# A triangle multiplication's b projection that takes tokens side by side, and a new issue order

## The chip, the cores and the metric

One core of a Trainium2 chip runs the whole program in one launch. The time is the device time of one execution in microseconds (us). In the trace the engines are PE (TensorE's matmuls), PEld (its weight loads), DVE (VectorE), ACT (ScalarE), POOL (GpSimd) and SP (SyncE, which here only issues transfers). L873 means line 873 of the kernel before.

## What is computed

Two layers over `x` of shape (32, 56, 56, 128), that is 32 images of 56 x 56 tokens with 128 channels, all float32:

```python
# layer 0
x = x + conv3x3(sign(batchnorm(_ln_c(x))), sign(W) * mean|W|)     # 128 -> 128 channels
t = x as (32, 3136, 128)
t = t + moe(_ln_t(t))               # router to 8 experts, best 2, softmax gates, 128 -> 128 each
# layer 1
x = x + triangle(_ln_c(x))
t = t + expert_choice(_ln_t(t))     # 64 experts; each takes its best 8 tokens of every image

def triangle(x):
    a = sigmoid((x @ Wa1 + ba1) * (x @ Wa2 + ba2))     # 128 -> 16
    b = sigmoid((x @ Wb1 + bb1) * (x @ Wb2 + bb2))     # 128 -> 16
    g = sigmoid(x @ Wg + bg)
    z = einsum('bikc,bkjc->bijc', a, b)                # rows of a by columns of b, per channel
    return g * (_ln(z) @ Wz + bz)
```

The change lies in the computation of `b` in `triangle`; the rest matters because it shares the engines.

## The kernel before

**Tiling.** Images go in 16 pairs. A pair's 2 x 56 rows are cut into 7 units of 16 rows (896 tokens), held as [128 partitions, 7, 128 channels] in float32. A row has 56 columns, counted as column = 7 v + n with v from 0 to 7 and n from 0 to 6: a partition holds the seven columns n of one (row, v). Turned (channels on partitions), a pair's normalised tokens lie in one buffer, `yT` [128, n = 7, row = 112, v = 8]. So, along a partition, the eight columns v of a row are neighbours, and a whole image of one n is 448 numbers in a row; a single column v over all rows has a step of eight numbers.

**Stages.** A first phase reads all of `x`, normalises, sums for the batch norm and loads the weights. Then each pair goes through these stages, at the names the trace uses:

- convolution: SP fetches `x` and `ys`; DVE writes signs into `frame` (L609); PE runs nine taps of 448 columns (`ps_cv`, L631); ACT scales (`cv`, L639); PE turns it back (`trc`); DVE adds;
- mixture of experts: statistics on DVE (`st`, then small steps ending in `rm`); ACT normalises (`ym`); PE turns (`trm`); ACT copies (`xT`); the router (`ps_rl`, `ps_r`) and its gates on DVE; PE turns the gates (`trg`), ACT copies and stores them to memory. For each of the seven blocks of a unit SP fetches the gates back, spread over all partitions (`gb`, 512 KB), DVE multiplies them onto the tokens (L825), and PE runs eight matmuls into `acc` (L830); DVE adds;
- triangle: statistics (`rmln`), ACT's norms (`yt`), PE's turn (`trt`), ACT's copies into `yT`; `tri_b` and `tri_a`; `tri_z`, the product per channel (`ps_z`, L972), its norm, and a way through memory into `zc`; `tri_out` with the gate matmuls (`ps_g`, L1063) and the output projection (`ps_zo`, L1085);
- expert choice: statistics, norms (`yl`), turn (`trl`), copies, logits (`ps_l`, ACT's copy of 128 x 448), DVE's MAX8 over all tokens of an image, index search, ACT's exponential over the logits (`top8`), the gathers on GpSimd. The experts' own matmuls and the scatters into the output (L1497, GpSimd) come when all pairs are through; only a part of them starts earlier.

**The projections a and b.** `gated_half` (L861 to L914) does one half (h = 0, 1) of one of them. For each of the two images it fills one PSUM bank: four matmuls (g = 0 to 3), each with the 128 x 32 weights into its own 32 partitions, 392 columns each. For `a` the moving operand is seven rows with all their columns, for each of the seven n a run of 7 x 8 = 56 neighbours. For `b` it is one column, v = 2 g + h, of all 56 rows and all seven n: 392 numbers eight apart. ACT adds the bias and writes the bank into `lines` (L882 for b, L887 for a), which lie as [(g, two times 16 channels), 7 slices, both images' rows at 0 and 64]. PE turns the seven slices (`tr_b`, `tr_a`; four into one bank and three into another); ACT copies the second factor (`abm`, L905), DVE multiplies it with the first (L910). Last, ACT's sigmoid writes `b_s` (L927) or `a_bd` (L945), the two operands of `ps_z`. So b has 2 halves x 2 images x 16 pairs = 64 banks and as many line copies; a has the same.

**What sets the order.** Nothing is left to the compiler's scheduler. Every operation is recorded with its engine, a planned cost in ns, what it reads and what it writes (`@op`). Its rank is the pair's number times 14 plus a number of the table `TICK` (L38 to L67), one number for each stage and unit. `Order.run` then plays the program in planned time: at each moment each engine takes, of the operations whose operands are ready by the plan and whose buffers are free, the one with the lowest rank. The instructions are issued in the order so found. On the chip each engine works through its own list strictly in that order. A changed cost or rank can thus move operations of any stage. The rotating buffers have fixed numbers: 8 PSUM banks, 12 of `x`, 5 of `u` (`ys`, `cv`, `ym`, `yt`, `yl`, `sg` and others share them), 5 of `gb`, 3 of `yl` (the turned `yl`), 2 of `abm`.

The sums that a mean over channels needs in the load of the weights use `mean_w`, a 128 x 128 matrix of 1/128 (L323, L324); it is read at L1775 and L1795.

Of the kernel before, what the change touches and what calls it, by code (L numbers as in the profile page):

```python
# [12 lines left out]
F32 = mybir.dt.float32  # L13
# [3 lines left out]
AF = mybir.ActivationFunctionType  # L17
# [21 lines left out]
    "fetch": (1.02, -3.61, 2.69, -0.51, 1.44, 9.95, 12.41),  # L39
    "sign": (-0.5, 1.65, 2.33, 6.44, 7.89, 10.12, 11.51),  # L40
    "conv": (2.3, 3.61, 7.1, 8.56, 10.24, 11.55, 14.66),
    "conv_back": (2.64, 3.67, 7.29, 8.6, 10.28, 12.05, 15.19),
    "moe_turn": (5.91, 4.92, 9.12, 9.24, 12.92, 12.75, 15.53),
    "moe_gates": (6.45, 6.7, 9.47, 10.57, 13.11, 13.01, 16.67),
    "moe_experts": (7.02, 7.48, 9.81, 10.77, 13.79, 15.45, 17.23),
    "moe_add0": (9.01, 10.3, 10.03, 12.99, 16.15, 17.26, 18.81),
    "moe_add1": (7.58, 10.23, 12.34, 12.06, 15.46, 16.15, 18.8),
    "tri_turn": (15.5, 16.45, 18.46, 17.26, 19.45, 19.21, 19.35),
    "moe_stats": (4.04, 8.64, 12.23, 15.22),
    "moe_route": (6.38, 9.37, 13, 15.78),  # L50
    "tri_stats": (14.95, 13.48, 18.14, 19.08),
    "tri_b": (19.69, 19.75),
    "tri_a": (19.7, 20.48),
    "tri_z": (21.12,),
    "tri_out": (23.16, 24.17, 24.33, 25.06, 26.73, 27.48, 29.06),
    "gate_stats": (24.67, 24.78, 28.01, 30.57),
    "gate_turn": (25.36, 25.49, 26.93, 28.7, 29.36, 30.77, 32.34),
    "gate_logits": (25.97, 26.82, 27.76, 30.12, 31.49, 34.49, 33.31, 33.27),
    "clear": (33.53,),
    "top8": (35.12,),  # L60
    "pool_rows": (35.94,),
    "late_first": (36.84, 37.89, 39.05, 42.18, 42.2, 42.46),
    "late_alone": (45.47, 44.2, 38.54, 42.56, 42.9, 46.32),
    "late_rest": (37.49, 37.53, 39.21, 40.16, 41.64, 41.88, 42.22, 43.47, 46.56, 47.54),
    "last_sums": (47.77,),
    "last_rows": (52.37,),
# [217 lines left out]
def kernel(ctx: ExitStack, tc: tile.TileContext, a: dict, out: bass.AP):  # L284
# [38 lines left out]
    mean_w = const.tile([128, 128], F32, name="mean_w")  # L323
    nc.gpsimd.memset(mean_w, 1.0 / C)  # L324
# [80 lines left out]
    with ExitStack() as c2:  # L405
# [18 lines left out]
        lines = [one.tile([128, N7, 128], F32, name=f"lines_{h}") for h in range(2)]  # L424
# [433 lines left out]

        all_rows = [("yT", u, n0) for u in range(NU) for n0 in (0, 4)]

        def gated_half(p, x, h, pieces, w, bias):  # L861

# [1152 lines left out]
```

## Time and profile before

| quantity | value |
|---|---|
| time, median of three runs | 3907.89 us (3904.44 to 3908.85) |
| time of the profiled execution | 3864.27 us |
| its span, first to last instruction | 3862.1 us |
| mean granted clock of TensorE in it | 0.960 |
| instructions in it | 78172 |
| experts' matmuls `acc` (L830) | 12544, 1462.6 us busy, 278 ns each |
| convolution taps `ps_cv` (L631) | 2016, 433.1 us, 361 ns each |
| gate products `gb` on DVE (L825) | 784, 952.9 us, 1223 ns each |
| norms `yt`, `yl`, `ym` on ACT (L560) | 784 each, 335.1, 329.4 and 315.5 us |
| scatters into the output (L1497) | 128, 198.1 us, 1548 ns each |
| memory traffic | 811.90 MB in packets, 209 GB/s over the span |

The span and all rows below it are of one profiled execution. The slices quoted below divide the span into 40 equal stretches; a digit is the busy share in tenths. A line of the timeline gives the start in us, the duration of a run of like instructions, engine, line, operation, output and inputs by name, the shape, the number of instructions, and in brackets the idle time of that engine before it with what ended it. In a line of the stretches, start and end are followed by the length, and each engine's busy us with the number of its instructions.

### The profile page before, as it was taken

The numbers are of one execution on the slowest core, as the hardware profiler recorded it, in microseconds if no ns is written. First come the engines' busy times: TensorE is split into PE (matmuls) and PEld (weight loads), VectorE is DVE, ScalarE is ACT, GpSimd is POOL, SyncE is SP. The second block draws the span as 40 slices with busy tenths as digits, with TensorE's granted clock in tenths as the row PEclk, the third lists the DMA queues.
The fourth block names the chain that finished last, engine by engine and source line by source line (L and its number), as shares of the span: only waits on it lengthen the run. The fifth ranks groups of instructions, "written<-read, shape, count | busy, mean of one in ns | idle before, by whom it ended". The sixth has DMA issues, their size and how long they took to land.

```text
span 3862.1 us, 78172 instructions
## 1 busy us (share of the span) xinstructions
PE 3515.1 (91%) x27693; PEld 2833.9 (73%) x27693; DVE 3142.5 (81%) x10452; ACT 2353.3 (61%) x5458; POOL 409.8 (11%) x472
## 2 busy tenths in 40 slices
PE   7999999999999999999999999999999999997673
PEld 6886787777777777777777778786868787865342
DVE  7997879898989898989898989898989898875310
ACT  5997446665756566666657575757575747565210
POOL 1000000000000000000000000000010101013657
PEclk8999999999999999999999999999999999987776
DMA  7996547565656565555556555655556565556784
GB/s 247 351 353 245 214 165 247 171 236 180 227 188 213 198 209 197 203 208 207 201 204 212 204 209 202 207 203 214 204 198 220 191 227 188 207 191 190 196 212 69
DMA packets 325542, 811.90 MB, mean 210 GB/s; under 512 B 86169, under 2 KB 110658, under 8 KB 325154
## 3 DMA queue, kind: packets, MB, share of 16 engines
q1 hardware_dynamic: 262034, 680.39, 51.2%
q10 hardware_dynamic: 41104, 109.20, 7.2%
q0 software_dynamic: 22016, 17.32, 3.0%
q8 instruction: 220, 3.60, 0.4%
q14 instruction: 168, 1.38, 0.1%
HBM read 630.19 MB, written 176.55 MB: 209 GB/s over the span
## 4 chain that ended last, share of the span: by engine, by line
PE 43%; DVE 20%; ACT 18%; DMA 13%; issue 3%; POOL 2%; SPq 0%; ACTq 0%; POOLq 0%; DVEq 0%
PE acc L830 28%; DMA gb<-gate 7%; DVE stln L486 5%; DMA out<-eo_False,picked 5%; ACT yt L560 3%; DVE sg L1098 3%; DVE gb L825 2%; PE ps_cv L631 2%; PE gram L1673 2%; DVE x L1107 2%; POOL out L1497 2%; ACT y L560 2%; ACT cv L639 2%; PE ps_z L972 2%; ACT ym L560 2%
## 5 line engine op out<-in xcount | busy, mean ns | idle before, releaser
L830 PE MATMUL acc<-expert_w,gb 128*128 128x128 f32 x12544 | 1462.6, 278 | 45.6 <-DVE gb L825 43.8
L830 PEld LDWEIGHTS acc<-expert_w,gb 128*128 128x128 f32 x12544 | 1434.2, 194 | 71.5 <-DVE gb L825 62.8
L825 DVE TENSOR_TENSOR gb<-gb,xT 128x1024 f32<-128x1024 f32 x784 | 952.9, 1223 | 95.6 <-DMA gb<-gate 93.2
L486 DVE BATCH_NORM_STATS2 stln<-x 128x6 f32<-128x128 f32 x2352 | 576.6, 287 | 1.5
L560 ACT ACTIVATE yt<-x,rmln 128x128 f32<-128x128 f32 x784 | 335.1, 493 | 212.6 <-DVE rmln L548 205.1
L631 PE MATMUL ps_cv<-frame,w_sign 128*128 128x448 bf16 x2016 | 433.1, 361 | 8.4 <-DVE frame L609 8.4
L560 ACT ACTIVATE yl<-x,rmln 128x128 f32<-128x128 f32 x784 | 329.4, 488 | 167.3 <-DVE rmln L545 157.3
L631 PEld LDWEIGHTS <-w_sign 128*128 128x128 bf16 x2016 | 193.2, 99 | 222.5 <-issue 66.5
L560 ACT ACTIVATE ym<-x,rmln 128x128 f32<-128x128 f32 x784 | 315.5, 485 | 56.7 <-DVE rmln L548 55.8
L1229 POOL DMA_INDIRECT rows<-y,near x128 | 124.1, 969 | 1148.5 <-PE trt L475 1040.7
L1114 POOL MEMSET a_bd<- 128x2048 f32 x16 | 29.5, 1842 | 1818.7 <-PE ps_zo L1085 1818.7
L1497 POOL DMA_INDIRECT out<-eo_False,picked x128 | 198.1, 1548 | 143.3 <-DMA out<-eo_False,picked 79.9
L581 ACT COPY xT<-trm 128x512 f32<-128x512 f32 x224 | 108.2, 536 | 163.4 <-PE trm L475 129.5
L639 ACT ACTIVATE cv<-ps_cv,cv_shift,cv_scale 128x448 f32<-128x448 f32 x224 | 159.5, 720 | 77.8 <-PE ps_cv L631 58.7
L560 ACT ACTIVATE y<-x,rm 128x128 f32<-128x128 f32 x448 | 194.8, 486 | 19.5 <-DVE rm L545 11.3
L1063 PE MATMUL ps_g<-wg,yT 128*128 128x128 f32 x1568 | 200.9, 280 | 0.0
L842 DVE TENSOR_TENSOR x<-acc,x 128x512 f32<-128x512 f32 x224 | 139.7, 624 | 74.5 <-PE acc L830 74.2
L486 DVE BATCH_NORM_STATS2 st<-x 128x6 f32<-128x128 f32 x784 | 180.6, 282 | 23.2 <-DMA x<-in_x 22.8
L1673 PE MATMUL gram<-y 128*128 128x128 f32 x1568 | 197.3, 278 | 0.0
L1673 PEld LDWEIGHTS gram<-y 128*128 128x128 f32 x1568 | 193.2, 199 | 0.0
L1063 PEld LDWEIGHTS ps_g<-wg,yT 128*128 128x128 f32 x1568 | 187.2, 194 | 8.2 <-PE pe_False L1471 0.8
L475 PE MATMUL tr<-ident,y 128*128 128x128 f32 x784 | 138.6, 294 | 27.5 <-ACT y L560 23.7
(244 smaller groups left out, 5305.4 us busy)
## 6 DMA issues: line engine op xcount, KB each, us to landing
gb<-gate SPq DMA_DIRECT2D x784, 512.0 KB
x<-in_x SPq DMA_DIRECT2D x224, 448.0 KB
y<-yT SPq DMA_DIRECT2D x112, 448.0 KB
ys<-y SPq DMA_DIRECT2D x112, 448.0 KB
out<-x ACTq DMA_DIRECT2D x112, 448.0 KB
y<-yl ACTq DMA_DIRECT2D x112, 448.0 KB
w_False<-in_L_ffn_weight SPq DMA_DIRECT2D x128, 256.0 KB
w_True<-in_L_ffn_weight SPq DMA_DIRECT2D x48, 256.0 KB
```

The source lines that it names most:

```text
L475: nc.tensor.transpose(ps.ap[:, n * 128 : (n + 1) * 128], get()[:, n0 + n, :], ident)
L486: nc.vector.bn_stats(st.ap[:, c0 + k, :], src.ap[:, k, :])
L560: nc.scalar.activation(dst.ap[:, k, :], src.ap[:, k, :], AF.Identity, bias=m, scale=r)
L631: nc.tensor.matmul(acc, lhsT=w_sign[:, tap, :], rhs=frames[f][:, 8 * band + kh : 8 * band + kh + 8, kw : kw + W], start=(tap == 0), stop=( ...
L639: nc.scalar.activation(cv.ap[:, :, 64 * h : 64 * h + 64], ps.ap[:, :448].rearrange("c (q n) -> c n q", n=N7), AF.Identity, bias=cv_shift, ...
L825: nc.vector.tensor_tensor(gb.ap, gb.ap, over(xT.ap[:, n, :], E0), ALU.mult)
L830: nc.tensor.matmul(acc.ap[:, n % 4 * C : (n % 4 + 1) * C], lhsT=gb.ap[:, e, :], rhs=expert_w[:, e * C : (e + 1) * C], start=(e == 0), stop ...
L842: nc.vector.tensor_tensor(dst, acc.ap[:, : k * C], dst, ALU.add)
L1063: nc.tensor.matmul(psg.ap[:, n * C : (n + 1) * C], lhsT=yT[:, n0 + n, 16 * u : 16 * u + 16, :].rearrange("c r v -> c (r v)"), rhs=wg, star ...
L1229: nc.gpsimd.indirect_dma_start(out=rows.ap[:, j, :], out_offset=None, in_=y3_d[p], in_offset=bass.IndirectOffsetOnAxis(ap=near.ap[:, k + j ...
L1497: ins = nc.gpsimd.indirect_dma_start(out=tokens_out, out_offset=bass.IndirectOffsetOnAxis(ap=picked[lot][:rows, e : e + 1], axis=0), in_=e ...
L1673: nc.tensor.matmul(gram.ap[:, :C], lhsT=y.ap[:, n, :], rhs=y.ap[:, n, :], start=(g % G16 == 0 and n == 0), stop=(g % G16 == G16 - 1 and n ...
```

## The change

The changed kernel computes the same. Five things differ.

1. **b's pieces.** Half h of b now takes the residues n = 4 h + g: four for h = 0, three for h = 1. One matmul takes all 448 neighbouring tokens of one n and one image. So the bank has 448 columns, in the second half on 96 partitions only. `lines` grow from 7 to 8 slices (one for each v), the turn makes four and four, `abm` holds [8, 4, 16]; the sigmoid writes the columns n = 0 to 3 or 4 to 6 of every v. The piece for g = 3 has its place on the array given explicitly. `a` keeps its form.
2. **`mean_w`** leaves the constants and becomes an operation of the weights' load in a buffer of the `yl` kind.
3. **Planned costs**: those of the projections (twice the columns plus 60 on PE, the columns plus 60 on ACT), the turns (20 + 130 k for k slices, instead of 125 k), `ps_z` (1880 for 1776), `ps_g` (40 more), `ps_zo` (680 for 900), `ps_l` (890 for 800), and one activation of the late experts (1850 for 1800).
4. **The table `TICK`** has new numbers throughout.
5. From costs and table, `Order.run` yields another order on every engine. In the steady state, for example, MAX8 stands ahead of the last step of unit 6's norm statistics on DVE, four `ps_l` stand ahead of the pair's last experts on PE, and 36 convolution matmuls instead of 18 stand ahead of the experts of units 2 and 3.

```diff
 TICK = {
...
-    "conv": (2.3, 3.61, 7.1, 8.56, 10.24, 11.55, 14.66),
+    "conv": (2.4, 3.69, 6.8, 7.72, 10.43, 11.89, 12.86),
...
-    "moe_experts": (7.02, 7.48, 9.81, 10.77, 13.79, 15.45, 17.23),
+    "moe_experts": (7.18, 7.67, 10.31, 10.83, 14.93, 12.94, 16.8),
...
-    "tri_b": (19.69, 19.75),
-    "tri_a": (19.7, 20.48),
-    "tri_z": (21.12,),
+    "tri_b": (19.79, 19.99),
+    "tri_a": (19.82, 21.57),
+    "tri_z": (21.72,),
...
-    "top8": (35.12,),
+    "top8": (34.46,),
...
-    mean_w = const.tile([128, 128], F32, name="mean_w")
-    nc.gpsimd.memset(mean_w, 1.0 / C)
...
-        lines = [one.tile([128, N7, 128], F32, name=f"lines_{h}") for h in range(2)]
+        lines = [one.tile([128, NV, 128], F32, name=f"lines_{h}") for h in range(2)]
...
-        def turned(src, name, keys=None, get=None):
+        def turned(src, name, keys=None, get=None, pieces=((0, 4), (4, 3))):
...
-            for n0, k in ((0, 4), (4, 3)):
+            for n0, k in pieces:
                 ps = bank(f"{name}_{n0}")
 
-                @op("PE", k * 125, r=keys or parts(src)[n0 : n0 + k], w=[ps])
+                @op("PE", 20 + k * 130, r=keys or parts(src)[n0 : n0 + k], w=[ps])
...
-        def gated_half(p, x, h, pieces, w, bias):
+        def gated_half(p, x, h, w, bias):
...
-            cols = x == "b"
             name = f"{x}_{p}_{h}"
+            if x == "a":
+                n_i, groups, size = N7, 4, 392
+            else:
+                n_i, groups, size = NV, (4, 3)[h], 448
+            rows = 32 * groups
             for img in range(2):
                 ps = bank(f"ps_{name}_{img}")
 
-                @op("PE", 830, r=all_rows, w=[ps])
+                @op("PE", 2 * size + 60, r=all_rows, w=[ps])
                 def _(ps=ps, img=img):
-                    for g in range(4):
+                    for g in range(groups):
+                        if x == "a":
...
+                        else:
+                            piece = yT[:, 4 * h + g, H * img : H * img + H, :].rearrange(
+                                "c r v -> c (r v)"
+                            )
+                            to = ps.ap[32 * g : 32 * g + 32, :size]
                         nc.tensor.matmul(
-                            ps.ap[32 * g : 32 * g + 32, :392].rearrange("s (n k) -> s n k", n=N7),
-                            lhsT=w, rhs=pieces(img, g), start=True, stop=True,
+                            to, lhsT=w, rhs=piece, start=True, stop=True,
+                            **({"tile_position": (0, 96)} if g == 3 else {}),
                         )
 
-                @op("ACT", 460, r=[ps], w=[("lines", h, img)])
+                @op("ACT", 60 + size, r=[ps], w=[("lines", h, img)])
...
+                        of = ps.ap[:rows, :size].rearrange("s (r v) -> s v r", v=NV)
+                    nc.scalar.activation(to, of, AF.Identity, bias=bias[:rows])
+
+            u = new("abm", [128, NV, 4, CH], f"abm_{name}")
...
-            u = gated_half(
-                p, "b", h,
-                lambda img, g: yT[:, :, H * img : H * img + H, 2 * g + h],
-                wb, bb,
-            )
+            u = gated_half(p, "b", h, wb, bb)
 
             @op("ACT", 540, r=[(u, 0), (u, 4)], w=[(b_s, h)])
             def _():
+                ns = slice(4 * h, min(4 * h + 4, N7))
                 nc.scalar.activation(
-                    b_s.ap.rearrange("p c (g z) -> p c g z", g=4)[:, :, :, 7 * h : 7 * h + 7],
-                    u.ap.rearrange("p i g c -> p c g i"), AF.Sigmoid,
+                    b_s.ap.rearrange("p c (v n) -> p c v n", n=N7)[:, :, :, ns],
+                    u.ap[:, :, : (4, 3)[h], :].rearrange("p v n c -> p c v n"), AF.Sigmoid,
                 )
...
-                @op("PE", 230 * k, r=[("yT", u, n0), ("zc", 0), ("zc", 1)], w=[psg])
+                @op("PE", 40 + 230 * k, r=[("yT", u, n0), ("zc", 0), ("zc", 1)], w=[psg])
...
-            @op("PE", 900, r=[("zc", 0), ("zc", 1), (sg, "s", 0)], w=psz)
+            @op("PE", 680, r=[("zc", 0), ("zc", 1), (sg, "s", 0)], w=psz)
...
-            @op("PE", 800, r=[k for yl in yls for k in parts(yl)], w=[ps])
+            @op("PE", 890, r=[k for yl in yls for k in parts(yl)], w=[ps])
...
+            mean_w = new("yl", [128, 128], "mean_w")
+
+            @op("POOL", 200, w=[mean_w])
+            def _():
+                nc.gpsimd.memset(mean_w.ap, 1.0 / C)
```

## The prediction, made before the changed kernel had run

> **What bounds the kernel.** I read the page first (engines and slices), then stages by windows, then one pair of images in order of time, then the waits of TensorE, and the chain that ended last.
>
> ```profile
> PE 3515.1 (91%) x27693; PEld 2833.9 (73%) x27693; DVE 3142.5 (81%) x10452; ACT 2353.3 (61%) x5458; POOL 409.8 (11%) x472
> ...
> PE   7999999999999999999999999999999999997673
> ```
>
> PE is full in all but the last four slices. The stages: 0 to 390 us (phase one, DMA share 0.98 in its middle) is not touched by the change; from 525 us each pair repeats, since the b projection starts at 524.94 us for the first pair and at 3462.43 for the sixteenth: 2937.5/15 = 195.8 us per pair; from 3509 us on GpSimd's serial scatters end the kernel (353 us), with PE busy 211 us of it. So a saving counts only as it shortens the 195.8 us. One such period, split where the pair's triangle product `ps_z` starts:
>
> ```profile
> 2271.00:2307.60 36.60, 34.21 (x232) 17.82 (x231) 26.83 (x83) 35.36 (x70) 9.35 (x9) 1.00 0.26 90
> 2307.60:2466.80 159.20, 151.63 (x1275) 132.99 (x1274) 145.81 (x461) 90.03 (x211) 1.81 (x1) 0.99 0.67 233
> ```
>
> After the window's length come busy us of PE, PEld, DVE, ACT and POOL. PE idles 9.9 us of 195.8. But in the first stretch, from the end of the experts to `ps_z`, ACT is as full as PE (35.4 of 36.6 us). There the b projection lies, and the change must be judged there.
>
> ```profile
> 2288.00 3.00 PE L873 MATMUL ps_b<-yT,wb 128*32 128x392 f32 x16
> ...
> 2290.80 1.52 PE L873 MATMUL ps_a<-yT,wa 128*32 128x392 f32 x16
> ...
> 2291.61 1.04 ACT L882 ACTIVATE lines<-ps_b,bb 128x392 f32<-128x392 f32 x2
> ...
> 2303.11 0.98 PE L475 MATMUL tr_a<-ident,lines 128*128 128x128 f32 x7 [2.00 <-ACT lines L887]
> ...
> 2305.13 2.03 ACT L945 ACTIVATE a_bd<-abm_a 56x448 f32<-56x448 f32 x2 [0.54 <-DVE abm_a L910]
> ```
>
> Two banks of b take PE 3.00 us, two of a 1.52, with the same 392 columns. But ACT takes up the b lines only at 2291.61, when the exp of the top-8 step is done; the b banks have been full since 2291. PE even waits 2.00 us for ACT's a lines later.
>
> **Part by part, PE.** b has 64 banks. Now 3.00/2 = 1.50 us each. With the eight columns contiguous, the nearest row is a's bank, 0.76 us for 392 columns, so 0.76 x 448/392 = 0.87 for 448. Ends: 1.50 x 448/392 = 1.71 if the speed stays the strided one; 0.65 for the half of the banks that drop from four groups to three, if groups cost in proportion (0.76 us on average). I take 0.87, a's row, since a reads runs of 56 contiguous numbers and the new b runs of 448. Saved: 64 x (1.50 - 0.87) = 40.3 us (ends: 13.4 lost, 47.4 gained). Added: 32 transposes, 31.5 us/224 = 0.14 each, 4.5 us. Net 35.8 us, 2.2 per pair.
>
> Here a rule speaks against the change. The Trainium skill, TensorE: Matmul & The Clock Gate, Part 2, step 3 (FILL), says throughput is purely N cycles, one column of the moving operand per cycle. 16 x 392 and 14 x 448 are the same 6272 columns per pair, so by the rule the projections save nothing and the transposes leave 4.5 us lost. The trace differs: same N, same type, same array strips, median instruction 882 ns for b and 492 for a; only the step between the numbers differs (eight apart, or side by side). The row decides; the rule stays as a rival.
>
> **DVE and ACT.** DVE: 32 products grow from 192 to 256 columns, 349 to 422 ns: 2.3 us, beside PE. ACT: 64 line copies grow from 392 to 448 (row of the gate logits' 128x448: 635 ns, against 582): 3.4 us; 32 copies 323 to 364 ns: 1.3 us; the sigmoids write 512 + 384 instead of 448 + 448: nothing. That is 0.3 us per pair in the stretch where ACT sets the end. The mean matrix moves into a rotating buffer and its fill into phase one's GpSimd queue: 0.2 us by the fill's own size, hidden by phase one's DMA (share 0.98), and some us of start if that cover were gone.
>
> **The order in that stretch.** T is the end of the pair's last expert matmul (2272.46). Before, `ps_z` starts at T + 35.1. In the new order:
> - the rstd of units 4 and 5 is finished on DVE before the sixth `gb` product of unit 6, not behind the seventh, so ACT's 14 norms `yt` of these units end about T; before, they started at T - 1.5 and spread to T + 14;
> - DVE's MAX8 (3.43 us) now stands ahead of the last step of unit 6's rstd. It waits for the last logits copy: PE needs 10 + 7 transposes and one `ps_l` (2.8 us), ACT three `xT` and two `yT` copies before it, T + 3.9. MAX8 ends at T + 7.5, and unit 6's norms, queued behind, start at T + 7.8 (before: rstd at T + 4.1). Then 7 norms (2.8), two `cv` (1.4), the turn and two `yT` copies (1.1): T + 13.1, against T + 14.7;
> - the table load and exp take 4.5 us, a `cv` moved ahead 0.7: b's lines start at T + 18.3, against T + 19.2. From there to the last a lines ACT took 11.4 us; less the moved `cv` 0.66, plus 0.46 for longer instructions: T + 29.5 against T + 30.6. Then 0.2 + 0.98 (`tr_a`) + 3.78 (two convolution bands before `ps_z`): T + 34.5.
>
> So the stretch shortens by only 0.6 us. PE's 2.2 us saved in it become waits for ACT. And four `ps_l` matmuls (0.55 each, 2.2 us) leave the stretch for a place ahead of the last experts: PE elsewhere grows by 2.2.
>
> **What the order takes from PE's waits elsewhere.** The period has 7 us of them outside the stretch. The largest:
>
> ```profile
> 2362.80 10.83 PE L830 MATMUL acc<-expert_w,gb 128*128 128x128 f32 x80 [0.80 <-DVE gb L825]
> ...
> 2392.64 2.05 PE L830 MATMUL acc<-expert_w,gb 128*128 128x128 f32 x16 [1.12 <-DVE gb L825]
> ...
> 2439.62 2.05 PE L830 MATMUL acc<-expert_w,gb 128*128 128x128 f32 x16 [1.98 <-DVE gb L825]
> ```
>
> The number in brackets is PE's wait. The experts of units 2 and 3 now come behind 36 convolution matmuls instead of 18, less one gate unit: 1.9 us more for their DMA, so 0.80 and 1.12 go. SP queues one `ys` more into that burst, 1.2 us of DMA, beside it. 0.38 (`trg`, now behind a `ps_zo`), 0.55 of 0.76 (`trc`, behind a router matmul) and 0.77 (`trt`, spread among convolutions) go too: 3.6 us. Against it, the next experts follow their gates by 9.7 us of PE work instead of 12.5; the first product was ready some 4 us early, so this costs between 0 and the 1.98 us of that place once more; I take 0.5. What is late next is ACT's router copy (1.15 us before `ps_r`), which keeps its place.
>
> **Sum.** Per pair -0.6 + 2.2 - 3.6 + 0.5 = -1.5; times 15 -22.5. The tail: the same PE work precedes the first scatter, the same 128 scatters follow, with one step of the last rows fewer behind them: -2. Together about -25 us: 3864.3 (span 3862.1 plus 2.2 around it) becomes 3839. The median of the runs is 3907.9, 43.6 us above the profiled one; I carry the difference over: **3883 us**.
>
> **Rivals.**
> 1. PE alone bounds: all 35.8 us arrive, and with the waits above some 10 more: 3908 - 45 = 3863. For it: PE 91%, DVE and ACT with slack over the period. Against: the stretch's ACT, row by row. Chance 0.33.
> 2. Hidden: ACT keeps the stretch, the waits only change places: 15 x 0.6 = 9 off, or less: 3903. For it: ACT waited for `ps_b` only 2.0 us in the whole trace. 0.10.
> 3. Slower, by the clock. After the 2.00 us wait in the stretch the granted clock fell in some pairs: 0.70 in the window 1125 to 1130 us, 1.00 in another pair. The new order splits more idle time among b and a (about 1.4 + 0.7 + 1.4 us). The skill's same page (Why this matters for your kernels) lets gaps up to about 3 us pass; by it the stretch is safe, by the row 2 us may suffice. A half-clock window, 3.4 us long, costs 1.7 us of PE; two more per pair cost 51 us, which overtakes the 25 from one per pair on: 3883 + 40 = 3923. 0.07.
> 4. The stride isn't b's price (the rule above): the 4.5 us, and no gain: about 3910. 0.03.
>
> The forecast has 0.47. About 0.2% (8 us) is what a measurement can tell from no change. Faster: forecast 0.46, rival 1 0.33, half of rival 2: 0.84; within 0.2%: 0.08; slower: 0.08. The range goes from rival 1 with a further 1 us per pair gained (3847) to rival 2: 3847 to 3904.
>
> **What would show it.** `ps_b` near 0.8 to 0.9 us a bank, median instruction near 550 ns; the period 194 to 194.5 us; ACT still full from the experts' end to `ps_z`, PE waiting for ACT's lines longer than 2.00 us; the `gb` waits of units 2 and 3 gone; first scatter to end again about 350 us. I am wrong if b's banks stay at 1.5 us, if the stretch shortens by 2 us or more, or if the clock's row shows more windows below 1.00.

## The result, and the profile after

| | before | after |
|---|---|---|
| median (us) | 3906.16 (4 runs, 3902.66 to 3908.85) | 3853.22 (4 runs, 3843.21 to 3860.09) |
| profiled execution (us) | 3864.27 | 3851.35 |
| its mean granted clock | 0.960 | 0.958 |
| period, one `ps_z` to the next, mean of 15 (us) | 196.09 | 195.20 |
| end of the experts to `ps_z`, mean (us) | 35.8 | 36.9 |
| `ps_z` to the end of the next experts, mean (us) | 160.2 | 158.2 |
| `ps_z` of the first pair (us) | 543.1 | 548.3 |
| last `ps_z` to the end (us) | 377.8 | 373.3 |

The ratio is 0.9863, with an interval of 0.9839 to 0.9887: 53 us less by the medians, where the prediction said 25. The time itself, forecast at 3883, lies in the range given. But the two profiled executions differ by only 12.9 us: 15 x 0.89 = 13.4 us from the periods, 4.5 from the tail, less 5.2 at the start. So there are two surprises: the runs gained twice the sum, the profiles half of it. The profiled execution of before, 3864, is not among its four runs, and lies 38 us below the lowest of them. "The stretch" below is the time from the end of a pair's last expert matmul to its first `ps_z`, "the rest" is what remains of the period.

The page after, engines (busy us, share of the span, instructions) and PE's 40 slices:

```profile
PE 3495.7 (91%) x27661; PEld 2836.7 (74%) x27661; DVE 3149.1 (82%) x10452; ACT 2355.4 (61%) x5458; POOL 407.0 (11%) x472
PE   7999999999999999999999999999999999997653
```

PE lost 19.4 us of busy time and is as full as before, by share. The two windows of the same pair as in the prediction, cut at the stretch's true ends (length, busy us of PE, PEld, DVE, ACT and POOL, clock, DMA share, GB/s):

```profile
2270.78:2309.14 38.36, 32.18 (x207) 17.37 (x206) 28.86 (x95) 30.18 (x56) 9.16 (x9) 0.91 0.20 47
2309.14:2467.05 157.91, 154.61 (x1308) 134.81 (x1308) 145.61 (x454) 95.58 (x224) 1.81 (x1) 1.00 0.69 245
```

In the stretch ACT is no longer full: 30.2 of 38.4 us (35.4 of 36.6 before). Neither is PE, and the stretch isn't shorter. Its granted clock is 0.91, where the same stretch of before showed 1.00; this becomes important below. Some lines of this pair's timeline:

```profile
2284.42 1.71 PE L886 MATMUL ps_b<-yT,wb 128*32 128x448 f32 x16
...
2285.95 1.50 PE L886 MATMUL ps_a<-yT,wa 128*32 128x392 f32 x16
...
2292.73 2.00 DVE L607 TENSOR_SCALAR frame<-ys,bn_scale,bn_limit 128x896 bf16<-128x896 f32 x1
...
2294.23 0.65 ACT L914 COPY abm_b<-tr_b 128x256 f32<-128x256 f32 x2 [2.25 <-PE ps_b L886]
...
2375.89 9.20 PE L828 MATMUL acc<-expert_w,gb 128*128 128x128 f32 x80 [0.19 <-DVE gb L823]
...
2442.30 9.20 PE L828 MATMUL acc<-expert_w,gb 128*128 128x128 f32 x80 [0.26 <-DVE gb L823]
```

Two banks of b take 1.71 us instead of 3.00. The experts' waits for `gb`, 0.80, 1.12 and 1.98 us in the lines of before, are down to 0.2 to 0.3. But ACT stands idle for 2.25 us before it copies `abm_b`, and the trace puts that down to PE. The profile of before has no such wait: there this copy started 22.2 to 22.7 us after the experts' end, here 23.45. That wait is where the experiments begin to matter.

### The profile page after: what moved, and what is told of

Its sections match the earlier page's. It is cut to its first block, busy times and chain, and to the rows that moved or that the text cites. A ratio compares the mean times of both kernels' runs of the same rounds, so it can differ in the third digit from the quotient of the medians.

```text
span 3849.5 us, 77967 instructions
## 1 busy us (share of the span) xinstructions
PE 3495.7 (91%) x27661; PEld 2836.7 (74%) x27661; DVE 3149.1 (82%) x10452; ACT 2355.4 (61%) x5458; POOL 407.0 (11%) x472
## 4 chain that ended last, share of the span: by engine, by line
PE 39%; DVE 33%; ACT 11%; DMA 9%; issue 4%; POOL 3%; ACTq 0%; another core or an unknown queue 0%; SPq 0%; DVEq 0%; POOLq 0%
PE acc L828 22%; DVE stln L484 8%; DVE gb L823 7%; DMA gb<-gate 4%; DVE sg L1098 3%; PE ps_cv L629 3%; DMA out<-eo_False,picked 3%; PE gram L1673 3%; POOL out L1497 2%; PE tr L473 2%; DVE x L1107 2%; DVE x L571 2%; ACT ym L558 1%; ACT yt L558 1%; PE ps_z L972 1%
## 5 line engine op out<-in xcount | busy, mean ns | idle before, releaser
L828 PE MATMUL acc<-expert_w,gb 128*128 128x128 f32 x12544 | 1443.9, 276 | 25.2 <-DVE gb L823 13.5
L828 PEld LDWEIGHTS acc<-expert_w,gb 128*128 128x128 f32 x12544 | 1415.1, 192 | 67.3 <-DVE gb L823 33.9
L558 ACT ACTIVATE yt<-x,rmln 128x128 f32<-128x128 f32 x784 | 324.5, 486 | 123.2 <-DVE rmln L546 120.0
L558 ACT ACTIVATE yl<-x,rmln 128x128 f32<-128x128 f32 x784 | 318.6, 487 | 125.9 <-DVE rmln L543 113.3
L1114 POOL MEMSET a_bd<- 128x2048 f32 x16 | 29.5, 1841 | 1846.3 <-PE ps_zo L1085 1400.7
L473 PE MATMUL tr<-ident,y 128*128 128x128 f32 x784 | 139.2, 295 | 29.1 <-ACT y L558 23.1
```

Of the source, the lines that this page charges most:

```text
L473: nc.tensor.transpose(ps.ap[:, n * 128 : (n + 1) * 128], get()[:, n0 + n, :], ident)
L558: nc.scalar.activation(dst.ap[:, k, :], src.ap[:, k, :], AF.Identity, bias=m, scale=r)
L828: nc.tensor.matmul(acc.ap[:, n % 4 * C : (n % 4 + 1) * C], lhsT=gb.ap[:, e, :], rhs=expert_w[:, e * C : (e + 1) * C], start=(e == 0), stop ...
```

## The experiments

Runs e1 to e4 were taken on one chip, called A here, e5 to e8 and e9 to e12 on another, B, e13 to e16 on C, e17 and e18 on D. Each ratio is to the kernel before, run beside them on the same chip. Means over pairs are over the first fifteen.

### Which part of the change brings the time: e1 to e4

e1 is the kernel before once more, e4 the changed kernel. e2 has the new b (and the moved `mean_w`) with the old order, e3 the old, strided b with the new order; both keep the other kernel's planned costs, so that the lists of PE, DVE and ACT are those of before (e2) or after (e3).

e2 against before has the diff of b shown ahead, without its costs, as here for the turns:

```diff
+                @op("PE", (4, 3)[n0 > 0] * 125, r=keys or parts(src)[n0 : n0 + k], w=[ps])
```

e3 against after:

```diff
-                            piece = yT[:, 4 * h + g, H * img : H * img + H, :].rearrange(
-                                "c r v -> c (r v)"
-                            )
+                            piece = yT[:, :, H * img : H * img + H, 2 * g + h]
```

> The kernel before, unchanged, profiled beside its own timed runs. The profile the prediction was summed on took 3864 us, the timed runs 3903 to 3909. If that execution was a stroke of luck, a new profile shows 3900 to 3910 and some place of the span is longer by 40 us in all (more half-clock windows than 16 in the steady part, or longer waits for gb); then the term 'carry the difference over' was the error. If profiled executions are always faster, it shows about 3864 again, and the change is worth only 13 us between profiles.

> b in eight-column pieces, but every engine's order as before. By the theory of the prediction ACT keeps the stretch before ps_z and b's cheaper banks become waits: 0 to 10 us off (ratio 0.9975 to 1.000). If PE alone bounds (rival 1), 36 us off or more: about 3870, ratio 0.991.

> The strided b with 392 columns, but every engine's order as in the changed kernel. By the theory of the prediction the order brings nearly all of it, 15 to 25 us by the waits for gb of units 2 and 3 (ratio 0.994 to 0.996), and with b's banks at 1.50 us again the stretch stays bound by ACT. If PE alone bounds, the strided banks cost their 36 us back, so only 10 to 17 us remain (ratio 0.996 to 0.9975). The whole change measured 0.9863; if neither part is worth half of 53 us alone, the two need each other.

> The changed kernel on the same chip and beside the same runs of before, so that the three can be set against it: ratio 0.984 to 0.989. If its profile shows the same stretches as the first one (195.2 us from ps_z to ps_z), then the difference between the profiles of before is before's own.

| chip A | median | ratio | stretch | PE idle in it | rest | PE idle in it |
|---|---|---|---|---|---|---|
| e1, before | 3875.2 | 1.0008 [0.9997, 1.0020] | 35.4 | 2.4 | 160.3 | 7.3 |
| e2, b alone | 3869.0 | 0.9994 [0.9986, 1.0003] | 35.8 | 4.6 | 160.2 | 7.0 |
| e3, order alone | 3847.2 | 0.9926 [0.9912, 0.9940] | 36.1 | 4.0 | 158.4 | 4.1 |
| e4, after | 3843.4 | 0.9919 [0.9905, 0.9934] | 36.1 | 5.8 | 158.1 | 3.8 |

b alone brings nothing that can be told from no change, though its banks are cheap and PE is busy 31 us less than in e1 (3471.5 against 3502.5). The window of its stretch, and of the changed kernel's two:

```profile
2273.64:2309.47 35.83, 30.73 (x216) 16.48 (x215) 26.91 (x82) 34.59 (x68) 9.29 (x9) 1.00 0.28 88
```

```profile
2271.38:2307.54 36.16, 31.50 (x207) 17.37 (x206) 28.96 (x89) 29.53 (x56) 9.24 (x9) 0.91 0.16 39
2307.54:2465.24 157.70, 154.71 (x1308) 134.92 (x1308) 146.23 (x461) 95.92 (x225) 1.81 (x1) 1.00 0.70 247
```

In e2 ACT is busy 34.6 of 35.8 us; PE has 2.2 us more idle time (4.6 for 2.4) and nothing else moves. In the waits of PE (us in total, times, longest), that is the line of `tr_b`, which grew from 7.8 us in e1 to:

```profile
PE tr_b L473 <- ACT lines L899: 30.2, 28, 1.8
```

The order brings nearly all (in e3 24 us by the medians and 29 by the ratio; 15 to 25 were expected), and in the rest of the period, where PE waits for the gate products; the same view of e1 and then of e4:

```profile
PE acc L830 <- DVE gb L825: 46.2, 46, 2.8
```

```profile
PE acc L828 <- DVE gb L823: 15.3, 47, 1.4
```

And on chip A the gain of the whole change is 28 us (31 by the ratio), near the sum of 25 and less than was expected of e4. So the missing half of the runs' gain isn't in the sum: it depends on the chip. The kernel before takes 3871 us here (median of 33 runs), and took 3906 in the first measurement; the changed one takes 3843 and took 3853.

### The changed kernel's stretch is not ACT's: e6 and e7

In all 16 pairs the exponential of the top-8 step goes over the first 448 of 3136 numbers only (the sum over the rest is left out), which takes 2.3 us from ACT's list ahead of b's lines: in e6 in the changed kernel, in e7 in the one of e3.

```diff
-                    lg.ap, lg.ap, AF.Exp, bias=q.ap[:, 0:1], accum_out=q.ap[:, 1:2]
+                    lg.ap[:, :448], lg.ap[:, :448], AF.Exp, bias=q.ap[:, 0:1],
+                    accum_out=q.ap[:, 1:2],
```

> The changed kernel, but the exponential of the top-8 step goes over 448 of the 3136 logits (the sum of the weights is that of these alone), same order: ACT has about 2.3 us less ahead of b's lines. Theory B (ACT holds the stretch): 2 us a pair, 30 us off. Theory A (DVE's sign operation holds it): ACT reaches the same wait for abm_b earlier, less than 10 us off.

> The same shortened exponential (448 of 3136 logits) in the kernel with the changed order and the strided b. If ACT holds the stretch there, too, 20 to 30 us off against the 3847 us of that order with the strided b; and less than the kernel with b's eight-column pieces gains if PE, with 2.4 us more of b, becomes the next bound.

e6 took 3852.2 us (0.9881 [0.9864, 0.9898]), e7 3855.2 (0.9893 [0.9876, 0.9910]); the changed kernel itself has 3850.1 on this chip (e12 below). So 2.3 us less of ACT's work per pair bring nothing in e6. For e7 the kernel of e3 has no run on this chip; its ratio is 0.3% below that of e3 on chip A, which doesn't decide. The window of e6:

```profile
2277.28:2315.53 38.25, 31.99 (x208) 17.25 (x206) 28.91 (x95) 27.89 (x56) 9.25 (x9) 0.91 0.19 45
```

ACT has 10.4 us idle and the stretch is as long as in e12 (38.26 us for the same pair). In the new order something else ends it, on this chip.

### DVE's sign operation beside GpSimd's fill: e5

The timeline of e4 from b's lines on:

```profile
2288.71 1.14 ACT L899 ACTIVATE lines<-ps_b,bb 128x448 f32<-128x448 f32 x2
...
2291.38 0.63 ACT L914 COPY abm_b<-tr_b 128x256 f32<-128x256 f32 x2
...
2292.23 3.14 DVE L607 TENSOR_SCALAR frame<-ys,bn_scale,bn_limit 128x896 bf16<-128x896 f32 x1
...
2292.94 1.61 POOL L1035 MEMSET zv<- 128x1792 f32 x1
...
2295.30 0.40 DVE L919 TENSOR_TENSOR abm_b<-tr_b,abm_b 128x256 f32<-128x256 f32 x1
...
2295.76 1.53 PE L886 MATMUL ps_a<-yT,wa 128*32 128x392 f32 x8 [1.52 <-DVE abm_b L919]
...
2296.32 1.08 ACT L933 ACTIVATE b_s<-abm_b 128x512 f32<-128x512 f32 x1 [2.84 <-DVE abm_b L919]
```

The new order puts one sign operation for the convolution (`frame`) ahead of the product `abm_b`. Its median over the kernel is 1.26 us; here, beside GpSimd's fill of `zv`, it takes 3.14, so the product comes 1.9 us late, and ACT (2.84 us) and PE (1.52 us) wait for it.

The same trace holds a comparison for it. In the second pair the fill comes only when the sign operation is through, and that has its 1.22 us. Set beside the fourteenth pair, which has the fill inside the sign operation, with the clock at 1.00 in both stretches:

```profile
710.93:745.21 34.28, 28.70 (x208) 16.03 (x206) 27.04 (x89) 29.57 (x56) 9.72 (x9) 1.00 0.17 38
3049.96:3086.17 36.21, 28.77 (x208) 16.05 (x206) 28.98 (x89) 29.57 (x56) 9.23 (x9) 1.00 0.15 39
```

```profile
731.79 1.22 DVE L607 TENSOR_SCALAR frame<-ys,bn_scale,bn_limit 128x896 bf16<-128x896 f32 x1
...
733.12 1.61 POOL L1035 MEMSET zv<- 128x1792 f32 x1
...
3070.82 3.15 DVE L607 TENSOR_SCALAR frame<-ys,bn_scale,bn_limit 128x896 bf16<-128x896 f32 x1
3071.53 1.61 POOL L1035 MEMSET zv<- 128x1792 f32 x1
```

PE and ACT do the same work in both, DVE is busy 1.94 us longer, and the stretch is 1.93 us longer. So on this chip the wait for the sign operation is worth 1.9 us in 13 of the 15 stretches, and without it the stretch takes 34.3 us, near the 34.5 of the prediction's list. e5 moves the sign operation behind the sixth product of the projections:

```diff
+            if self.stage(k) == "sign" and self.stage(dve[i + 1]) == "gated_half":
+                products = [j for j in dve[i + 1 :] if self.stage(j) == "gated_half"]
+                at = out.index(products[5])
...
+                out.remove(k)
+                out.insert(at, k)
```

> The changed kernel with one DVE operation per pair moved: the sign operation (frame, 3.14 us at this place against 1.26 us elsewhere) stands behind the products abm_b of half 1 instead of ahead of those of half 0. Theory A (this operation holds the products, and ACT's sigmoid b_s waits 2.84 us and PE's ps_a 1.52 us for them): the stretch shortens by 2 to 2.8 us a pair, 30 to 40 us in all, and frame is back at 1.26 us. Theory B (ACT alone holds the stretch, as the prediction had it): the idle time only changes places, 0 to 8 us off.

Measured: 3857.9 us (0.9904 [0.9887, 0.9921]), no gain against e12's 3850.1 on the same chip, where 30 to 40 us were expected; it was not run on chip A. In its trace the sign operation is back at 1.26 us, but ACT copies `abm_b` only 23.3 us after the experts' end, as in the first profile of the changed kernel. This chip has another, later wait, and that one decides.

### What is late on chips B and C: e8 and e12

Both kernels were run again without an edit, on the chip of e5 to e7.

> The kernel before once more, beside the others. If the level of 3906 us belongs to some chips (the first measurement) and 3872 us to others, this shows one of the two, and the profile beside it shows in which stretches 35 us lie; the other kernels of this call then show whether the new order is as sensitive (first measurement 3853, second 3843 us).

> The changed kernel beside them, as the measure for the second kernel of this call: if before stands near 3900 here, the ratio is about 0.986 to 0.988, as in the first measurement; if it stands near 3872, about 0.992, as in the second.

e8 took 3895.7 us (0.9994 [0.9983, 1.0006]), e12 3850.1 (0.9888 [0.9870, 0.9906]). Their periods are 197.81 and 194.90 us; 15 x 2.91 = 44 us, the gain of the runs here. Against chip A the kernel before has lost 1.9 us of each stretch (37.4 for 35.4), the changed one 0.5 (36.6 for 36.1). The kernel before on chip A (e1) and on chip B (e8), at the same place of the same pair:

```profile
2291.12 0.98 PE L475 MATMUL tr_b<-ident,lines 128*128 128x128 f32 x7 [0.39 <-ACT lines L882]
...
2293.11 0.20 ACT L772 ACTIVATE d<-d 128x14 f32<-128x14 f32 x1
2293.13 0.94 POOL L1229 DMA_INDIRECT rows<-y,near  x1 [0.30 <-issue]
2293.21 0.57 ACT L905 COPY abm_b<-tr_b 128x256 f32<-128x256 f32 x2
...
2294.06 1.63 POOL L1035 MEMSET zv<- 128x1792 f32 x1
```

```profile
2307.96 0.98 PE L475 MATMUL tr_b<-ident,lines 128*128 128x128 f32 x7 [0.40 <-issue]
...
2309.95 0.20 ACT L772 ACTIVATE d<-d 128x14 f32<-128x14 f32 x1
2310.00 0.95 POOL L1229 DMA_INDIRECT rows<-y,near  x1 [0.31 <-issue]
2310.95 1.61 POOL L1035 MEMSET zv<- 128x1792 f32 x1
2312.60 0.59 ACT L905 COPY abm_b<-tr_b 128x256 f32<-128x256 f32 x2 [2.45 <-PE ps_b L873]
```

In e1 the turn `tr_b` is done at 2292.10, and ACT copies right behind its step `d`. In e8 the turn is done at 2308.94 and `d` at 2310.15, yet the copy starts at 2312.60: 24.75 us after the experts' end, where e1 has 22.20. What it waits for is PE's word that the turn is done. The times at which PE's semaphore updates (the words for which other engines wait) appear in the trace, in us after the end of the experts, for the same pair of four kernels with the old order and three with the new one:

```
e1   17.04  18.44  20.78  21.11  22.66  24.06  24.70  25.02
e8   18.92  24.73  24.78  24.87  24.97
e9   18.95  24.77  24.82  24.92  25.01
e11  17.04  18.98  20.78  21.11  22.66  24.07

e4   14.65  15.40  16.06  16.70  16.75  19.19  19.63  20.53  21.28  22.32
e12  14.65  18.87  23.14  23.21  23.25  23.32
e13  14.64  17.42  17.51  17.59  17.63  19.18  19.62  20.52  21.27  22.31
```

In e8, updates due between 20.8 and 24.1 all come together at 24.7 to 25.0. Just then the row of eight gathers of the top-8 step and the fill behind them are over on GpSimd (23.1 and 24.7 us after the experts' end). Over the whole execution the waits of ACT have one line in e8 that e1 doesn't have:

```profile
ACT abm_b L905 <- PE ps_b L873: 35.8, 14, 2.7
```

35.8 us in 14 pairs: more than the 25 us by which the two chips differ for this kernel. The trace has the difference: in e1, six of the fifteen stretches have 3.4 us at half clock (granted clock 0.50) on the convolution's matmuls ahead of `ps_z` and are 1.65 us longer for it, 10 us in all; in e8 the half-clock time falls into PE's waits and costs next to nothing. In e12 the same wait exists, as two lines (23.6 and 19.4 us); but there the late word meets the sign operation's wait. In e4, with updates in time, the first product `abm_b` starts 23.9 us after the experts' end; in e12, with late ones, at 23.9 too. So the changed kernel loses only the 0.5 us, as the means over the pairs show.

### The gathers hold the updates, the fill doesn't: e9, e10, e11, e13

e9 (against before) and e10 (against after) take the fill of `zv` from GpSimd and let ACT write it in the previous stage. e11 (before) and e13 (after, chip C) leave out four of the eight gathers in all pairs but the last, and fill the rows with zeros instead; e16 is the changed kernel without an edit on chip C.

e9 and e10:

```diff
+                nc.scalar.activation(
+                    zv.ap.rearrange("p v j h -> p (v j h)"),
+                    yT[:, :2, :, :].rearrange("c n r v -> c (n r v)"),
+                    AF.Identity, bias=1.0, scale=0.0,
+                )
...
-                nc.gpsimd.memset(zv.ap, 1.0)
```

e11 and e13:

```diff
+                        if k and p < NP - 1:
+                            nc.gpsimd.memset(rows.ap[:, j, :], 0.0)
+                            return
```

> The kernel before, with the fill of zv (ones, 128x1792, 1.61 us) taken from GpSimd, where it follows the eight row gathers, to ACT behind its square of z; every other instruction in its old order. In the slow executions of before (3892 us span) four semaphore updates of PE, due from 20.8 us after the experts' end on, came together at 24.7, when GpSimd's fill ended; in the fast ones (3860) they came in time. Theory C (GpSimd's fill holds them): where before stands near 3900, this one is 1.6 to 2.5 us a pair faster, 24 to 38 us; where before stands near 3872, within 5 us of it. Theory D (the gathers hold them, the fill only ends last): no more than 1 us a pair.

> The same move of the fill in the changed kernel. Theory C: the sign operation on DVE, 2.0 to 3.14 us beside the fill, is back near 1.26 us and ACT's copies of abm_b start near 20 us after the experts' end instead of 23.4; 15 to 40 us off against the changed kernel. Theory D: within 10 us of it.

> The kernel before, where four of the eight row gathers of each pair but the last are replaced by small fills of zeros (those rows are left out of the pooled sums); the fill of zv stays on GpSimd. Theory D (gathers hold PE's updates): GpSimd is through 4 us earlier, and where before stands near 3900 this one is about 35 us faster; near 3872, within 5 us. Theory C (the fill): the fill comes 4 us earlier, too, beside the exponential, where PE's updates are not on the path: also faster where before is slow; the two differ in whether updates are held during the four gathers left.

> The changed kernel with four of the eight row gathers of each pair but the last replaced by small fills of zeros (those rows are left out of the pooled sums). In the changed kernel two things end together near 24 us after the experts' end: DVE's sign operation beside GpSimd's fill, and, where before stands near 3900, PE's held updates. With four gathers neither should be there: abm_b copies near 20 us, the sign operation at 1.26 us. If both only cover each other, 25 to 40 us off against the changed kernel, wherever before stands; if the stretch is then held by ACT's row of work, under 10 us.

> The changed kernel beside them: 0.986 to 0.989 of before where before stands near 3900 us, about 0.992 where it stands near 3872.

| | median | ratio | stretch | `abm_b` starts (after the experts' end) |
|---|---|---|---|---|
| e9, before, no fill | 3893.5 | 1.0003 [0.9992, 1.0013] | 37.4 | late, as in e8 |
| e10, after, no fill | 3848.6 | 0.9880 [0.9864, 0.9896] | 36.6 | late, as in e12 |
| e11, before, four gathers | 3881.3 | 0.9955 [0.9940, 0.9971] | 35.6 | 22.25 |
| e13, after, four gathers | 3827.5 | 0.9835 [0.9819, 0.9850] | 35.2 | 20.0 |
| e16, after | 3842.9 | 0.9871 [0.9852, 0.9890] | 36.5 | late, as in e12 |

Without the fill the updates stay late, at 24.77 us in e9 as in e8. The line of ACT's waits in e9 is that of e8, too:

```profile
ACT abm_b L905 <- PE ps_b L873: 35.7, 14, 2.7
```

So the fill falls as their cause. What both traces record up to 24.7 is the landing of the last gather (24.3 to 24.8). With four gathers the updates for which ACT waits come on time in both kernels, and e11's stretch is that of chip A. It isn't that four gathers hold nothing: in e13 the updates due at 15.4 to 16.8 come at 17.4 to 17.6. But the row is over before those that matter are due. Four gathers also let the fill come some 4 us earlier, but e9 and e10 have shown that the fill alone doesn't matter to the updates. In the runs e11 gains 13 us where 35 were expected: its stretches are 1.7 us shorter than e8's in the mean, 26 us in all (six of fifteen have half-clock windows ahead of `ps_z` again), but the rest of the period is 0.6 us longer, 9 us in all, and the tail 2 us. In e10 the sign operation is back at 1.26 us and nothing is gained, because the late updates remain; in e5 it was the same. e13 has both gone, and gains 15 us against e16, where 25 to 40 were expected if nothing else held the stretch and under 10 if ACT did. The waits of ACT in e13 still show a third, short one:

```profile
ACT b_s L933 <- DVE abm_b L919: 13.5, 14, 1.1
```

In e4 this line has 37.9 us. What holds e13 back is the clock: five of its fifteen stretches have no half-clock time and take 34.3 us, nine have it in the convolution's matmuls ahead of `ps_z` and take 36.0.

### The gathers split, with the whole computation: e14, e15, e17

Four of the eight gathers are moved behind the second product of b, and the sums over their rows behind the last product (e14). e15 also takes the fill to ACT. e17 is e15 with the late sums behind the norm statistics of the next experts (and the turn of the summed rows one `ps_z` later); e18 is the changed kernel without an edit beside it.

e14 against after:

```diff
+            moved[b[1]] = gathers[8 * p + 4 : 8 * p + 8]
+            moved[b[7]] = sums[8 * p + 4 : 8 * p + 8]
```

e17 against e15:

```diff
-            moved[b[7]] = sums[8 * p + 4 : 8 * p + 8]
+            first = next(j for j, k in enumerate(dve) if at[k] > at[b[7]] and stage(k) == "moe_experts")
+            moved[dve[first - 1]] = sums[8 * p + 4 : 8 * p + 8]
```

> The changed kernel, complete, but the gathers in two lots of four: the second lot's row numbers are written by DVE only behind the first products abm_b, and the sums and copies that need its rows stand behind the products of a. If five and more gathers in a row hold PE's updates and four do not, abm_b is copied near 20 us after the experts' end; the fill of zv now comes behind the second lot, away from the sign operation. 15 to 40 us off against the changed kernel; if the second lot holds the updates of a's lines in its turn, nothing or a loss of some us a pair.

> The same two lots, and the fill of zv on ACT behind its square of z. As the kernel with two lots, with zv ready independently of the second lot: the same time within 5 us, or 5 to 15 us less if the fill behind the second lot came too late for the way of z through memory.

> The two lots of gathers with the fill of zv on ACT, and the four sums of the second lot moved behind the next units' norm statistics on DVE (ahead of them they made ym start 1.9 us later, and the time from ps_z to the next experts' end grew by 1.2 us a pair). If that was all that ate the gain of the split, the stretch stays at 34.3 to 36.0 us and the rest falls back to about 158.3: 1.2 us a pair, 10 to 20 us off against the changed kernel beside it. If it does not fall back, the second lot of gathers costs something else there, and the time is the changed kernel's within 6 us.

> The changed kernel beside it, as its measure: 3840 to 3855 us.

| | median | ratio | stretch | rest |
|---|---|---|---|---|
| e16, after, chip C | 3842.9 | 0.9871 [0.9852, 0.9890] | 36.5 | 158.2 |
| e14, split gathers, C | 3849.4 | 0.9890 [0.9869, 0.9911] | 35.3 | 159.4 |
| e15, with the fill on ACT, C | 3844.0 | 0.9880 [0.9860, 0.9900] | 34.8 | 159.6 |
| e18, after, chip D | 3847.9 | 0.9914 [0.9894, 0.9934] | 36.3 | 158.6 |
| e17, sums later, D | 3833.3 | 0.9885 [0.9866, 0.9904] | 35.6 | 158.3 |

e14 and e15 are misses that teach: the stretch shortens as it should, by 1.2 to 1.7 us, and the rest takes it back, because the late sums stand on DVE ahead of the statistics of the next experts' norms. These end 2.6 us (e14) and 2.9 us (e15) behind the first `ps_z`, against 1.2 us in e16 (means of pairs 2 to 14). With the sums behind them (e17) they end with it, the rest is as short as in the changed kernel, and e17 is 14.6 us below it on the same chip. It gives the whole output and is the fastest complete version here; it was not run on B or C. The waits for the product `abm_b` in e17, and in e18:

```profile
ACT b_s L973 <- DVE abm_b L954: 13.4, 14, 1.0
```

```profile
ACT b_s L933 <- DVE abm_b L919: 37.9, 14, 2.9
...
PE ps_a L886 <- DVE abm_b L919: 17.5, 13, 1.5
```

On chip D the updates of the changed kernel come in time (e18 has no wait of `abm_b` for `ps_b`), so here it's the sign operation's wait that e17 removes. The 1.9 us in 13 pairs would be 25; 14.6 arrive. The clock takes most of the difference. Two stretches of e17, one after the other:

```profile
1872.60:1906.89 34.29, 28.48 (x206) 15.89 (x204) 26.01 (x86) 29.55 (x54) 7.56 (x8) 1.00 0.29 89
2064.70:2100.65 35.95, 30.14 (x206) 16.46 (x204) 27.45 (x93) 29.97 (x54) 7.55 (x8) 0.95 0.31 102
```

With the clock at 0.95 the same matmuls keep PE busy 1.66 us longer, and the stretch is 1.66 us longer. Thirteen of the fourteen full stretches are of the second kind.

## Why the prediction was half right

**The cost of b's bank: right.** 0.87 us were predicted from a's row, 1.71/2 = 0.855 were measured at full clock, and the median instruction went from 882 to 539 ns:

```profile
L886 PE MATMUL ps_b<-yT,wb x448: 536/539/957, 528.2 to 3463.1; 128*32 128x448 f32 x150
```

So rival 4 (the stride isn't the price) falls, and with it the rule of one column per cycle that it rested on. The lower end, three groups cheaper than four, is out as well: two three-group banks take 1.70 us (e13).

**"PE's 2.2 us saved in it become waits for ACT": right.** e2 shows it, by 2.2 us of new idle time on PE and no gain. Rival 1, that all of PE's saving arrives, falls with it: PE is busy 31 us less in e2, near the 35.8 of the sum, and the runs don't show it.

**The gb waits: right in size.** 3.6 us of PE's waits outside the stretch were to go; 7.3 became 3.8 (e1 and e4). PE's own work there grew by 1.3 us and not 2.2, and the 0.5 us for gates that follow closer don't show, so the rest of the period lost 2.2 us where the sum had 3.6 - 2.2 - 0.5 = 0.9. Of the 0.9 us of PE's work that didn't come, some 0.7 is the clock: behind fewer waits the rest of the fifteen periods has 2 half-clock windows (of 3.4 us each) in e4 and 8 in e1.

**The stretch: wrong.** 0.6 us less were predicted, 0.7 more came on chip A. The list on ACT was followed well: b's lines start 17.3 us after the experts' end (18.3 predicted), and where nothing disturbs it the stretch takes 34.3 us (34.5 predicted). What failed is that the sum went on along ACT alone, "From there to the last a lines". DVE's sign operation in front of the product wasn't costed there, and it took 3.14 us instead of 1.26 beside the fill; `ps_z` came at 36.1. The parts, from e1 to e4: 35.0 to 34.3 by the list, 1.9 us more by the sign operation, and some 0.4 us less because six stretches of e1 and two of e4 are lengthened by half clock. ACT no longer sets the end: it is busy 29.5 of e4's 36.2 us, where the profile after should have shown it "still full", and e6 shows the same on chip B. The errors of +1.3 us here and -1.3 us in the rest cancel, by luck, and the period from `ps_z` to `ps_z` changed from 195.96 to 194.27 us, by 1.7 (1.5 predicted).

**Start and tail.** The first `ps_z`, not costed, comes at 545 to 553 us in five profiles of the changed kernel and at 542 to 544 in three of the one before; 1 to 2 us of it are the first pair's longer stretch, and the remainder wasn't followed. The tail, with 2 us predicted, changed by -4.5, +0.6 (e1 and e4) and -6.6 us (e8 and e12).

**The step that failed for the time: "The median of the runs is 3907.9, 43.6 us above the profiled one; I carry the difference over".** It takes the difference for something that the kernel doesn't touch. For the changed kernel it measured 1.9 us (3853.2 against 3851.4). Part of it is a wait in the very stretch that the change rearranges. The first profile of before was of an execution with PE's updates in time. On chips B and C they are late, and that costs the kernel before 1.9 us of each stretch (e8 against e1) and the changed one 0.5 (e12 against e4), because in the new order the sign operation stands in the same place. So there the change is worth 15 x 1.4 = 21 us more by the profiles, and by the ratios 0.3 to 0.5%, 12 to 19 us:

| chip | updates in the changed kernel's trace | before | ratio of the changed kernel |
|---|---|---|---|
| A | in time (e4) | 3871.3 | 0.9919 [0.9905, 0.9934] |
| D | in time (e18) | 3880.5 | 0.9914 [0.9894, 0.9934] |
| B | late (e12) | 3899.3 beside e5 to e8, 3894.0 beside e12 | 0.9888 [0.9870, 0.9906] |
| C | late (e16) | 3891.9 | 0.9871 [0.9852, 0.9890] |

The first profile of the changed kernel had late updates, that of before had not, which is why the two profiles differ by 12.9 us only. The runs of before at 3906 have no trace; that their updates were late is inferred from their level, which is nearest to chips B and C, and isn't shown. With the 12 to 19 us, the 28 of chip A become 40 to 47 of the 53 us; the remainder stays open. Nor is it shown what makes a chip late: each chip here is known by one or two groups of runs, in which all traces agree. Some gap is there within one chip, too: e1's profiled execution, 3861.8 us at a clock of 0.964, is the lowest of its 13, and their median lies 13 us above it.

**The clock (rival 3): its sign came, its cost didn't.** The mean granted clock over the runs on chip A is 0.9600 before and 0.9598 after, and the changed kernel is faster, not slower. But the half-clock windows did move where the rival said: the fifteen stretches have 6 of them in e1 and 18 in e4, the rest of the periods 8 and 2. So one of the prediction's own signs of being wrong was there, and waits of 2.0 to 2.5 us were followed by half clock (last section), as its row had it and the rule of 3 us beside it had not. In e4 most of them fall where PE waits for the sign operation's product anyway. When that wait goes, in e13 and e17, the windows are what the stretch has left over its 34.3 us. (The rival's 3883 + 40 doesn't follow from its own 51 us, which would give 3934.)

## What to carry to other kernels

Before you carry the gap between a profiled execution and the runs over to a changed kernel, ask where in the period the gap could be: if it can lie in the stretch that the change rearranges, give the prediction both values. Follow a stretch over all the engines that hand work to each other in it, not along the fullest one alone; an operation moved in front of a product is priced by what runs beside it at its new place. Before rebuilding an operation that is slow on the busiest engine, look who waits for it: here 31 us of PE's time brought nothing (e2), and moving the work between two bursts brought the gain. And look at the clock stretch by stretch: an equal mean hid that the half-clock windows had moved into the stretch under repair.

## What the hardware showed that was not expected

- Eight GpSimd gathers in a row, 0.95 us each and 1.25 apart, go with PE's semaphore updates coming up to 3.9 us late on two of four chips (from 20.8 to 24.7 us after the experts' end, e1 against e8), with the copies behind them 2.5 us late. They come together 1.6 to 1.7 us after the last gather has ended, with a fill behind it (e8, e12) or without (e9, e10). Four in a row hold them as well, but only until some 0.9 us after the fourth (17.4 us in e13). PE itself goes on, `tr_b` and the next `ps_b` one behind the other as in e1; the other engines wait. On the two late chips the gathers' own landings are scarce in the trace, too: about 4 of 16 updates for each gather (e8, e12), against about 15 on chip A (e1, e4). By which path the gathers do it (their descriptors, or the traffic of their landings) is open.
- The sign operation on DVE is slower beside a fill on GpSimd: 1.26 us alone, 2.00 with 1.15 us of common time (the changed kernel's first profile), 3.14 with all of the 1.61 us fill inside it (e4). Whichever began first, in all 13 cases of e4 and all 13 of that profile it ended 0.8 to 0.9 us behind the fill, and the fill kept its 1.6 us. The Trainium skill, SBUF — State Buffer, section "SBUF: two separate sides", tells of an exclusive lock between GpSimd and those DVE operations that work in a two-port mode or have two inputs in SBUF: the first comer holds it for its whole instruction while the other blocks. Whether the sign operation is of that kind no run here shows. In e4 it came first by 0.7 us and still lost 1.9; the measurement decides.
- A wait of PE of some 2.5 us was followed by 3.4 us at half clock in 13 of 14 stretches of e17, one of 1.8 us in 6 of 14, one of 2.0 us in 6 of 14 of e1. Such a window costs 1.65 us when matmuls that `ps_z` stands behind fall into it, and nothing when it falls into another wait.
